# Adding the weights onto the low-rank part by accumulating transfers from GpSimd's queue instead of by a GpSimd sum

## Chip, core and metric

The kernel runs on one core of one Trainium2 chip. The metric is the device time of one launch in microseconds (us). Before the change it is 2744.04 us, the median of three runs (2742.25 to 2744.21).

The engines are named as in the profile: PE (TensorE, matrix products), DVE (VectorE), ACT (ScalarE), POOL (GpSimd) and SP (SyncE, which here only issues transfers). "SPq", "ACTq" and "POOLq" are the transfers that those engines issue.

## What is computed

The reference quantizes a weight matrix with a low-rank addition to the nearest of 32 codebook values, group by group, multiplies by it, and passes the result through a second linear layer with a small mixture of experts:

```
lora_delta = lora_B @ lora_A * (32.0 / 64.0)
scale      = exp(scale_log)                        # one per row and group of 128 columns
normalized = (weight + lora_delta).reshape(O, I // 128, 128) / scale
idx        = searchsorted(thresholds, normalized)  # 31 thresholds, 32 values
quantized  = cb[idx]
w          = (quantized - normalized) + normalized
w_eff      = (w * scale).reshape(O, I) + lora_delta
h          = x @ w_eff.T                           # x: 4096 x 2048, w_eff: 2048 x 2048
out        = x + ffn(h)                            # W_base, bias, router, experts
```

All of it is in float32. The change is in the sum `weight + lora_delta`.

## The kernel before

The kernel has two stages. Stage 1 (to about 1210 us of the span) builds the product of the two weight matrices, so that stage 2 has to multiply `x` only once; it does that with a two-level Strassen scheme and PE sets its pace. The change is in stage 1 alone.

**Strips.** Stage 1 goes over 16 strips of 128 columns. For strip `i` there is a tile `w_i` (128 partitions x 16 groups x 128, 1 MB), which becomes the normalized weight, and a tile `a_i` of the same size, which becomes the quantized weight and then PE's stationary operand. Each strip is handled in two halves `f` of 8 groups (128x1024 elements). There are two buffers for `w`, three for `a`, two for the mask `above`, and one in PSUM for the low-rank product `d`.

**One strip's quantization** is 28 steps (line 460; the lowest three thresholds are done elsewhere). In each step ACT writes a mask `above` = relu(w - threshold) (L462) and DVE copies the next codebook step into `a` where the mask is not zero (L463). With two masks, ACT can write the mask of step k+2 only when DVE has finished the copy of step k.

**Everything else is threaded between the steps.** The scheduler is off (`manual_schedule`), so the order of each engine's queue is the order of the program. `behind(k, ...)` puts work behind step k of the running strip i (k = 0 to 27): on ACT it then stands after the mask of step k, on DVE after its copy, on PE, POOL and SP just in that order. What is put there while strip i is quantized:

- PE: `delta(i+1, 0)` at the start and `delta(i+1, 1)` at step 7 (L408): the low-rank product of the next strip's halves, both into the one PSUM tile `d`, so that half 1 has to wait until half 0 has been read. Between them the products of strip i-1 with the second weight matrix (L526, `products`, at steps 2, 5, 8, 11, then 17, 20, 22), the first of which waits for POOL's line 479 of strip i-1. The tiles of `m` have three PSUM buffers, so a new one waits for ACT to copy an old one out (L545, `keep`, at steps 5, 6, 17 and 19).
- SP: `load_w(i+1)` (L343, 1 MB) at step 3, and the pieces of the second weight matrix (L395).
- ACT: `scaled(i+1, 0)` at step 7 and `scaled(i+1, 1)` at step 11 (L424), which copy 0.5 x `d` from PSUM into the halves of `a_{i+1}`.
- POOL: `normalize(i+1, 0)` at step 8 and `(i+1, 1)` at step 11: `w += a` (L431), then `w *= 1/scale` (L433).
- ACT: `level_0(i+1, f)`, three instructions for the lowest threshold (L441, L444, L446), at steps 10, 12, 14 for half 0 and 16, 18, 20 for half 1. L441 reads the normalized `w`, so it waits for L433. POOL then does the next two thresholds (`more_levels`, L453 and L454, at steps 14 and 20).
- After the strip, POOL's `straight_through(i)` (L477 to L479, three instructions for each half).
- While strips 5 to 14 run, POOL also makes a block of stage 2's operands: `outer_w` at step 4 (L280, four instructions), two `inner_pair` at step 9 (L289 to L292, eight instructions) and two more at step 15. SP stores them (L311 to L313). Strip 15 makes two such blocks, but has no next strip.

Strip 0 is started on its own: its low-rank part is added by DVE (L429), before the loop. `load_w(0)` and `load_w(1)` are issued at the start of the kernel (L360, L363).

Of the kernel before, what the change touches and what calls it, by code (L numbers as in the profile page):

```python
# [9 lines left out]
F32 = mybir.dt.float32  # L10
# [4 lines left out]
ALU = mybir.AluOpType  # L15
# [4 lines left out]
P = 128  # L20
BIG = 3.0e38
LORA_SCALE = 32.0 / 64.0
# [100 lines left out]
def exp_exact(nc, work, out, x):  # L123


    shape = list(x.shape)
    v = nc.vector
    v.tensor_scalar(x, x, -87.0, 88.0, ALU.max, ALU.min)
    k = work.tile(shape, F32, name="exp_k")
    half = 1.5 * 2.0**23  # L130
    v.tensor_scalar(k, x, 1.44269504088896341, half, ALU.mult, ALU.add)
    v.tensor_scalar(k, k, half, None, ALU.subtract)
    r = work.tile(shape, F32, name="exp_r")
    v.scalar_tensor_tensor(r, k, -0.693359375, x, ALU.mult, ALU.add)
    v.scalar_tensor_tensor(r, k, 2.12194440e-4, r, ALU.mult, ALU.add)
    y = work.tile(shape, F32, name="exp_y")
    v.tensor_scalar(y, r, 1.9875691500e-4, None, ALU.mult)
    for c in (1.3981999507e-3, 8.3334519073e-3, 4.1665795894e-2, 1.6666665459e-1, 5.0000001201e-1):
        v.scalar_tensor_tensor(y, y, c, r, ALU.add, ALU.mult)
    v.tensor_tensor(y, y, r, ALU.mult)  # L140
    v.tensor_tensor(y, y, r, ALU.add)

    bits = work.tile(shape, I32, name="exp_bits")
    v.tensor_scalar(bits, k, 127.0, float(1 << 23), ALU.add, ALU.mult)
    v.scalar_tensor_tensor(out, y, 1.0, bits.bitcast(F32), ALU.add, ALU.mult)
# [3 lines left out]
def adaln_ffn_kernel(  # L149
# [29 lines left out]
    nc = tc.nc  # L179
    D, N = xT.shape  # L180
    NS, _, NM, _ = weight.shape
# [34 lines left out]
    strip = [j * NK + k for k in range(NK) for j in range(4)]  # L216
# [44 lines left out]
    def columns(g, b, up, more):  # L261
        cols[g, b] = {
            "up": up.rearrange("p (j b a c) -> p j b a c", j=4, b=2, a=2),
            "more": more.rearrange("p (j b a c) -> p j b a c", j=3, b=2, a=2),
        }
# [50 lines left out]
    with ExitStack() as sa:  # L316
# [10 lines left out]
        wpool = sa.enter_context(tc.tile_pool(name="wpool", bufs=2))  # L327
# [11 lines left out]
        strips = {}  # L339

        def load_w(i):
            w = wpool.tile([P, NM, P], F32, tag="w", name=f"w_{i}")
            nc.sync.dma_start(w, weight[strip[i]])  # L343
            strips.setdefault(i, {})["w"] = w

        def load_la(i):
            la = lap.tile([2 * R, P], F32, tag="la", name=f"la_{i}")
            for h in range(2):
                nc.sync.dma_start(la[h * R : h * R + R], lora_A[:, ts(strip[i], P)])
            strips.setdefault(i, {})["la"] = la  # L350

        with tc.tile_pool(name="tables", bufs=1) as tables:
            log = tables.tile([P, NS * NM], F32, name="log")
            nc.scalar.dma_start(log, scale_log.rearrange("p s m -> p (s m)"))
            for h in range(2):
                nc.scalar.dma_start(
                    lora_BT_sb[h * R : h * R + R], lora_BT.rearrange("r (f h n p) -> r h f n p", h=2, n=4, p=P)[:, h]
                )
            nc.sync.dma_start(cb, codebook.partition_broadcast(P))
            load_w(0)  # L360
            for i in range(3):
                load_la(i)
            load_w(1)  # L363
            exp_exact(nc, tables, scale.rearrange("p s m -> p (s m)"), log)
            nc.vector.reciprocal(rscale, scale)
            neg_t, step, base = quantizer_tables(nc, tables, const, psum_t, cb)
# [47 lines left out]
        def half(i, f, t):  # L414
            return strips[i][t][:, ts(f, NM // 2), :]

        def new_a(i):
            strips[i]["a"] = apool.tile([P, NM, P], F32, tag="a", name=f"a_{i}")

        def scaled(i, f):  # L420

            if f == 0:
                new_a(i)
            nc.scalar.mul(half(i, f, "a"), strips[i]["d"], LORA_SCALE)  # L424

        def normalize(i, f):
            w = half(i, f, "w")
            if i == 0:
                nc.vector.scalar_tensor_tensor(w, strips[i]["d"], LORA_SCALE, w, ALU.mult, ALU.add)  # L429
            else:  # L430
                nc.gpsimd.tensor_tensor(w, w, half(i, f, "a"), ALU.add)  # L431
            r = rscale[:, strip[i], ts(f, NM // 2)]
            nc.gpsimd.tensor_tensor(w, w, r.unsqueeze(2).to_broadcast([P, NM // 2, P]), ALU.mult)  # L433

# [171 lines left out]
        def products(i, bs, c):  # L606

            for b in bs:
                multiply(i, b, c)
            if c == NC - 1:  # L610
                low_rank(i, bs)
# [9 lines left out]
        for i in range(NS):  # L621
            at = {}

            def behind(r, f, *args):
                at.setdefault(r, []).append(lambda: f(*args))

            if i > 1:

                products(i - 2, (3, 1), NC - 1)
                route(i - 2)  # L630
                behind(5, keep, i - 2, 3)
                behind(6, keep, i - 2, 1)
            if i + 1 < NS:
                delta(i + 1, 0)
                if i > 0:
                    behind(3, load_w, i + 1)
                behind(7, scaled, i + 1, 0)
                behind(8, normalize, i + 1, 0)
                for f, (a, b, c) in enumerate(((10, 12, 14), (16, 18, 20))):
                    behind(a, level_0, i + 1, f, 0)  # L640
                    behind(b, level_0, i + 1, f, 1)
                    behind(c, level_0, i + 1, f, 2)
                    behind(c, more_levels, i + 1, f)
                behind(11, scaled, i + 1, 1)
                behind(11, normalize, i + 1, 1)
            if i > 0:


                behind(9, load_route, i - 1)
                for c in range(2):  # L650
                    behind(2 + 3 * c, products, i - 1, (2, 0), c)
                if i + 1 < NS:
                    behind(7, delta, i + 1, 1)
                for c in range(2, NC):
                    behind(2 + 3 * c, products, i - 1, (2, 0), c)
                behind(13, multiply_router, i - 1)
                behind(17, keep, i - 1, 2)
                behind(19, keep, i - 1, 0)
                for c in range(NC - 1):
                    behind((17, 20, 22)[c], products, i - 1, (3, 1), c)  # L660
                behind(22, keep_router, i - 1)
                if i + 2 < NS:
                    behind(20, load_la, i + 2)
            else:
                behind(7, delta, i + 1, 1)
                behind(22, lora_columns, 0)
                behind(24, lora_columns, 1)
                behind(26, lora_router)
            for n, (g, b) in enumerate(made.get(i, [])):
                step_of = (4, 9, 11, 12, 15, 26, 27) if len(made[i]) == 1 else (  # L670
                    (4, 6, 8, 9, 10, 12, 13) if n == 0 else (17, 19, 21, 22, 23, 25, 26)
                )

                def begin(g, b):
                    columns(
                        g, b,
                        ypool.tile([P, 2048], F32, tag="up", name=f"up_{g}_{b}"),
                        ypool.tile([P, 1536], F32, tag="more", name=f"more_{g}_{b}"),
                    )
                    fetch(g, b)  # L680

                def inner_pair(g, b, ms):
                    z = zp.tile([P, 1024], F32, tag="z", name=f"z_{g}_{b}_{ms[0]}")
                    inner_some(nc.gpsimd, g, b, ms, z)

                behind((0, 14)[n], begin, g, b)
                r = step_of
                behind(r[0], outer_w, nc.gpsimd, g, b)
                behind(r[1], inner_pair, g, b, PAIRS[0])
                behind(r[1], inner_pair, g, b, PAIRS[1])  # L690
                behind(r[2], put, g, b, PAIRS[0])
                behind(r[3], put, g, b, PAIRS[1])
                behind(r[4], inner_pair, g, b, PAIRS[2])
                behind(r[4], inner_pair, g, b, PAIRS[3])
                behind(r[5], put, g, b, PAIRS[2])
                behind(r[6], put, g, b, PAIRS[3])
            quantize(i, at)
            straight_through(i)
# [448 lines left out]
```

## Time and profile before

One profiled execution took 2743.94 us, of which 2742.2 us are the span that the profile covers.

| | value |
|---|---|
| time, median of 3 runs | 2744.04 us |
| time of the profiled execution, its span | 2743.94 us, 2742.2 us |
| granted TensorE clock, mean | 0.967 |
| POOL busy over the span | 1244.1 us (45%) |
| DMA engines' mean share of queue 1 (SP) | 60.0% |
| POOL's sums L431 `w<-w,a`, 128x1024 | 30 of 2376 ns, 71.3 us |
| POOL's L433 `w<-w,rscale`, 128x1024 | 32 of 1896 ns, 60.7 us |
| ACT's L424 `a<-d`, 128x1024 | 30 of 1002 ns, 30.1 us |

The last three rows are groups of instructions by line, engine and tiles: how many there are, the mean duration of one, and the busy time together. How to read the views: a group's row ends with the idle time of its engine just before its instructions and with what ended that idle time. The list of waits says who waited for whom, with the total, the number of times and the longest. The timeline gives the instructions in order of time; an "x8" is eight merged ones, and brackets hold the idle time before. In the timeline an engine's next instruction often starts slightly before the last one's printed end.

### The profile page before, as it was taken

The numbers are of one execution on the slowest core, as the hardware profiler recorded it, in microseconds if no ns is written. First come the engines' busy times: TensorE is split into PE (matmuls) and PEld (weight loads), VectorE is DVE, ScalarE is ACT, GpSimd is POOL, SyncE is SP. The second block draws the span as 40 slices with busy tenths as digits, with TensorE's granted clock in tenths as the row PEclk, the third lists the DMA queues.
The fourth block names the chain that finished last, engine by engine and source line by source line (L and its number), as shares of the span: only waits on it lengthen the run. The fifth ranks groups of instructions, "written<-read, shape, count | busy, mean of one in ns | idle before, by whom it ended". The sixth has DMA issues, their size and how long they took to land.

```text
span 2742.2 us, 26226 instructions
## 1 busy us (share of the span) xinstructions
PE 2566.7 (94%) x10544; PEld 1766.2 (64%) x10544; DVE 1588.7 (58%) x993; ACT 1118.2 (41%) x741; POOL 1244.1 (45%) x699
## 2 busy tenths in 40 slices
PE   1599999999999999999599999999999999999999
PEld 0244444444444444445488888888888888888887
DVE  7999999999999999972433222332222422223321
ACT  3888989898888888840000000000000000000000
POOL 1666668888888888730203231032320323301314
PEclk9799999999999999999799999999999999999999
DMA  6345556767676666697954567545485455754564
GB/s 225 123 177 185 176 178 216 243 231 244 232 246 229 228 228 215 228 307 241 316 205 149 200 210 267 183 175 209 169 306 185 169 206 178 269 207 175 181 199 166
DMA packets 239913, 581.06 MB, mean 212 GB/s; under 512 B 18312, under 2 KB 140560, under 8 KB 194736
## 3 DMA queue, kind: packets, MB, share of 16 engines
q1 hardware_dynamic: 236848, 565.50, 60.0%
q10 hardware_dynamic: 2016, 11.14, 1.1%
q0 software_dynamic: 928, 2.75, 0.3%
q8 instruction: 83, 1.36, 0.2%
q14 instruction: 38, 0.31, 0.0%
HBM read 477.62 MB, written 101.71 MB: 211 GB/s over the span
## 4 chain that ended last, share of the span: by engine, by line
PE 56%; DVE 24%; ACT 10%; DMA 4%; issue 3%; SPq 3%; POOL 1%; DVEq 0%; POOLq 0%; ACTq 0%
PE z L805 48%; DVE a L463 22%; ACT above L462 7%; PE m L526 5%; PE z L835 1%; SPq L313 1%; ACT sg L441 1%; SPq L311 1%; SPq L312 1%; ACT sg L444 1%; ACT a L446 1%; ACT out L545 1%; DMA s_dram<-z 1%; DMA wbp<-in_wbT 0%; DMA first<-wc_dram 0%
## 5 line engine op out<-in xcount | busy, mean ns | idle before, releaser
L463 DVE COPY_PREDICATED a<-above,step 128x2048 f32<-128x2048 uint16 x449 | 1112.5, 2481 | 48.6 <-ACT above L462 5.7
L462 ACT ACTIVATE above<-w,neg_t 128x2048 bf16<-128x2048 f32 x449 | 895.2, 1999 | 127.9 <-DVE a L463 124.4
L805 PE MATMUL z<-t,s 128*128 128x256 f32 x3584 | 791.4, 380 | 0.4 <-DMA s<-s_dram 0.4
L805 PEld LDWEIGHTS z<-t,s 128*128 128x128 f32 x3584 | 678.3, 190 | 102.9 <-issue 12.5
L526 PE MATMUL m<-wbp,a 128*128 128x512 f32 x1024 | 505.2, 640 | 43.8 <-POOL a L479 35.2
L526 PE MATMUL m<-wb,a 128*128 128x512 f32 x1024 | 468.8, 601 | 26.9 <-ACT out L545 26.8
L526 PEld LDWEIGHTS m<-wbp,a 128*128 128x128 f32 x1024 | 205.7, 206 | 294.0 <-issue 242.8
L526 PEld LDWEIGHTS m<-wb,a 128*128 128x128 f32 x1024 | 195.5, 192 | 277.9 <-issue 239.2
L885 ACT COPY m<-z 128x1024 f32<-128x1024 f32 x28 | 28.4, 1013 | 769.8 <-PE z L805 769.8
L805 PE MATMUL z<-xA,s 128*128 128x256 f32 x1152 | 260.2, 385 | 33.5 <-DMA s<-s_dram 33.5
L805 PEld LDWEIGHTS z<-xA,s 128*128 128x128 f32 x1152 | 222.7, 194 | 66.0 <-issue 35.0
L896 POOL TENSOR_TENSOR c<-u,m 128x1024 f32<-128x1024 f32 x16 | 50.1, 3130 | 442.9 <-DVE u L893 400.4
L453 POOL TENSOR_SCALAR lv<-w,base 128x1024 f32<-128x1024 f32 x60 | 226.7, 3778 | 3.6
L896 POOL TENSOR_TENSOR M<-u,m 128x1024 f32<-128x1024 f32 x8 | 25.6, 3205 | 363.0 <-DVE u L893 358.3
L805 PE MATMUL z<-xC,s 128*128 128x256 f32 x768 | 169.7, 379 | 0.0
L805 PE MATMUL z<-xB,s 128*128 128x256 f32 x768 | 169.7, 379 | 0.0
L887 DVE TENSOR_TENSOR u<-z,m 128x1024 f32<-128x1024 f32 x28 | 34.2, 1223 | 218.6 <-issue 175.1
L805 PEld LDWEIGHTS z<-xB,s 128*128 128x128 f32 x768 | 146.1, 190 | 19.7
L805 PEld LDWEIGHTS z<-xC,s 128*128 128x128 f32 x768 | 146.0, 190 | 19.7
L891 ACT COPY m<-z 128x1024 f32<-128x1024 f32 x28 | 28.3, 1011 | 308.5 <-PE z L805 308.5
L454 POOL TENSOR_TENSOR a<-a,lv 128x1024 f32<-128x1024 f32 x60 | 142.5, 2375 | 18.5 <-ACT a L446 13.9
L477 POOL TENSOR_TENSOR a<-a,w 128x1024 f32<-128x1024 f32 x30 | 71.3, 2376 | 142.8 <-DVE a L463 142.8
(178 smaller groups left out, 1886.2 us busy)
## 6 DMA issues: line engine op xcount, KB each, us to landing
s<-s_dram SPq DMA_DIRECT2D x196, 1024.0 KB, 4.8
wbp<-in_wbT SPq DMA_DIRECT2D x131, 1024.0 KB, 5.2
xs<-in_xT SPq DMA_DIRECT2D x64, 512.0 KB, 7.1
xA<-in_xT SPq DMA_DIRECT2D x24, 1024.0 KB, 9.0
s_dram<-z SPq DMA_DIRECT2D x84, 256.0 KB, 5.6
w<-in_weight SPq DMA_DIRECT2D x16, 1024.0 KB, 7.4
xB<-in_xT SPq DMA_DIRECT2D x16, 1024.0 KB, 7.9
outT<-M SPq DMA_DIRECT2D x16, 1024.0 KB, 10.3
```

Of the source, the lines that this page charges most:

```text
L311: q.dma_start(to[:, n, 1:3, g, c], y[:, n, 1])
L453: v.tensor_scalar(lv, half(i, f, "w"), base[:, c + 1 : c + 2], base[:, c : c + 1], ALU.is_gt, ALU.mult)
L454: v.tensor_tensor(a, a, lv, ALU.add)
L462: nc.scalar.activation(above, q, AF.Relu, bias=neg_t[:, r : r + 1])
L463: nc.vector.copy_predicated(a, above.bitcast(U16), step[:, r : r + 1].to_broadcast([P, F]))
L477: v.tensor_tensor(a, a, w, ALU.subtract)
L526: nc.tensor.matmul(ps, strips[i]["a"][:, CM * c + m, :], t[:, m, :], start=c == 0 and m == 0, stop=False)
L805: nc.tensor.matmul(z[:, c, :], s[:, k, ts(c, P)], rhs[:, k, :], start=not more and k == 0 and c % PER == 0, stop=k == NK - 1 and c % PER = ...
L885: nc.scalar.copy(temp("m1", o), z["a"])
L887: nc.vector.tensor_tensor(temp("u2", o), z["b"], state["m1", o], ALU.add)
L891: nc.scalar.copy(temp("m5", o), z["c"])
L896: lambda d: nc.gpsimd.tensor_tensor(d, state["u3", o], state["m5", o], ALU.add),
```

## The change

`load_w` for strips 1 to 15 goes away, together with POOL's sum L431. ACT now writes the scaled low-rank part into `w` itself, and a transfer issued by POOL adds the 512 KB of the half's weights onto it. There are 30 such transfers, two for each of the strips 1 to 15. The buffer of `w_{i+1}` is taken when `scaled(i+1, 0)` runs. POOL's queue holds the issue where `scaled` stands; `normalize` keeps only the multiplication, which waits for the transfer.

Some of the steps change: `scaled(i+1, 1)` goes from step 11 to 9, `normalize(i+1, 0)` from 8 to 10, and `level_0(i+1, 0)` from steps 10, 12, 14 to 12, 14, 15 (with `more_levels(i+1, 0)` going from 14 to 15). Half 1's steps of `level_0` stay. Behind the diff, lines after 424 are two higher than before: the mask is L464, the copy L465, the multiplication by 1/scale L435, the scaled copy L425 and the transfer L426.

```
             load_w(0)
             for i in range(3):
                 load_la(i)
-            load_w(1)
...
             if f == 0:
                 new_a(i)
-            nc.scalar.mul(half(i, f, "a"), strips[i]["d"], LORA_SCALE)
+                strips[i]["w"] = wpool.tile([P, NM, P], F32, tag="w", name=f"w_{i}")
+            w = half(i, f, "w")
+            nc.scalar.mul(w, strips[i]["d"], LORA_SCALE)
+            nc.gpsimd.dma_start(w, weight[strip[i]][:, ts(f, NM // 2), :], accum_op=ALU.add)
...
             if i == 0:
                 nc.vector.scalar_tensor_tensor(w, strips[i]["d"], LORA_SCALE, w, ALU.mult, ALU.add)
             else:
-                nc.gpsimd.tensor_tensor(w, w, half(i, f, "a"), ALU.add)
+                pass
...
                 delta(i + 1, 0)
-                if i > 0:
-                    behind(3, load_w, i + 1)
                 behind(7, scaled, i + 1, 0)
-                behind(8, normalize, i + 1, 0)
-                for f, (a, b, c) in enumerate(((10, 12, 14), (16, 18, 20))):
+                behind(10, normalize, i + 1, 0)
+                for f, (a, b, c) in enumerate(((12, 14, 15), (16, 18, 20))):
...
-                behind(11, scaled, i + 1, 1)
+                behind(9, scaled, i + 1, 1)
                 behind(11, normalize, i + 1, 1)
```

## The prediction

> **What bounds the kernel now.** I read the groups of the page first, then the waits of stage 1 (0 to 1200 us), then one strip in the timeline, then the transfers. The two costliest groups:
>
> ```profile
> L463 DVE COPY_PREDICATED a<-above,step 128x2048 f32<-128x2048 uint16 x449 | 1112.5, 2481 | 48.6 <-ACT above L462 5.7
> L462 ACT ACTIVATE above<-w,neg_t 128x2048 bf16<-128x2048 f32 x449 | 895.2, 1999 | 127.9 <-DVE a L463 124.4
> ```
>
> DVE's copies take 1112.5 us. The 48.6 us of idle time before them are 0.1 us for each of 449 and 5.7 us of waiting for a mask. So stage 1 is DVE copying without a gap, and everything else fits in beside it. The waits say the same from the other side:
>
> ```profile
> POOL a L477 <- DVE a L463: 142.8, 15, 11.1
> ACT above L462 <- DVE a L463: 123.3, 235, 0.7
> PE m L526 <- ACT out L545: 31.1, 21, 2.1
> DVE a L463 <- ACT above L462: 5.7, 19, 0.7
> ```
>
> POOL is idle for 8 to 11 us at the end of every strip until DVE is done. ACT waits for DVE 0.5 us at a time: a copy comes every 2.58 us, a mask takes 2.00. ACT therefore can do about 1.1 us of other work between two masks before a copy is late, and gains back about 0.6 us in each step. Now the strip that starts at 486.1 us (rows out of the timeline of all engines):
>
> ```profile
> 486.12 2.38 POOL L477 TENSOR_TENSOR a<-a,w 128x1024 f32<-128x1024 f32 x1 [8.78 <-DVE a L463]
> ...
> 497.81 1.90 POOL L479 TENSOR_TENSOR a<-a,scale 128x1024 f32<-128x1024 f32 x1
> 498.17 0.57 ACT L545 COPY out<-m 128x512 f32<-128x512 f32 x1
> ...
> 498.78 3.70 PE L526 MATMUL m<-wb,a 128*128 128x512 f32 x8 [2.08 <-ACT out L545]
> ...
> 503.32 1.01 ACT L424 ACTIVATE a<-d 128x1024 f32<-128x1024 f32 x1
> 503.49 1.30 POOL L280 TENSOR_TENSOR more<-up,more 128x512 f32<-128x512 f32 x1
> ...
> 506.60 2.00 ACT L462 ACTIVATE above<-w,neg_t 128x2048 bf16<-128x2048 f32 x1 [0.39 <-DVE a L463]
> ...
> 509.28 1.16 PE L408 MATMUL d<-la,lora_BT_sb 64*128 64x128 f32 x16
> ...
> 511.10 1.13 ACT L441 ACTIVATE sg<-w,neg_t 128x1024 bf16<-128x1024 f32 x1
> ...
> 514.03 1.00 ACT L424 ACTIVATE a<-d 128x1024 f32<-128x1024 f32 x1
> ```
>
> I count from the strip's start: 486.1 is 0. POOL's straight-through ends at 13.6 and `outer_w` at 18.7. ACT scales half 0 at 17.2 (step 7) and half 1 at 27.9 (step 11). PE makes the second `d` from 23.2 to 24.3, far ahead of step 11. It can't be earlier: PE's queue holds before it two rounds of products, and the second product waits until ACT has copied an old tile out at step 5 (12.0 to 12.6), then needs 3.5 + 7.0 us of PE.
>
> **The change part by part.**
>
> *Removed: POOL's 30 sums, 30 x 2.376 = 71.3 us.* Worth 0: POOL waits for DVE at the end of every strip in any case, and DVE's waits for the whole chain over ACT are 5.7 us, which bounds the gain. *Removed: SP's load at step 3 and the one at the start.* Worth 0: SP issues in 0.35 us; at the start DVE's tables, not a transfer, decide until 32.7 us.
>
> *Moved: `scaled(.,1)` from step 11 to step 9.* ACT's mask of step 9 ends at 508.5, that is 22.4, and the next instruction is now the scaled copy, which needs the `d` that PE finishes at 24.3. Step 7's copy released that PSUM tile long before; it is PE's products that are late. So ACT waits 1.9 us, copies until 25.4, and only then writes the mask of step 10, ready at 27.3. DVE wants it at ten copies after the start, 10 x 2.577 = 25.8. The copy is 1.55 us late. PE starts this `d` 23.0 to 23.4 after the start of the strip in ten of the strips 1 to 14, at 23.9 in strip 1, and at about 25 in strips 4, 9 and 14, where a product runs slowly (5.40 us for 3.70). Sum: 14 x 1.55 = 21.7, and 0.8 + 0.5 + 2.0 + 1.7 + 1.7 = 6.7 for the late ones: **28.4 us**. Strip 0 has no products before its `d`: 0.
>
> *Added: issues on POOL.* The trace has 16 transfers issued by POOL, of 0.55 to 0.95 us each on its queue; I take 0.75. The first issue has room (17.2 + 1.0, or 18.7 behind `outer_w`). The second waits for ACT until 25.4, and in strips 5 to 14 two `inner_pair` (eight instructions from 510.15 to 515.90: 5.75 us) stand behind it, and behind them the multiplication of half 0. So: 25.4 + 0.75 + 5.75 + 1.90 = 33.8 for a normalized half 0. ACT reaches `level_0` at step 12, some 31.7 after the start with the delay above counted in. It waits 2.1 us; that the copy of step 13 is late by 1.85 follows as before. 10 x 1.85 = **18.5 us**. In strips 1 to 4 there is no `inner_pair`, and half 0 is ready when its transfer has landed.
>
> *Moved: `level_0`.* Steps 15 and 16 now hold 1.13 and 1.03 us of ACT back to back instead of with a step between. By the rule above (1.1 us to spare, 0.6 back in each step) the copies of steps 16, 17, 19 and 21 are late by about 0.75 together; the same count over the old order gives 0.4, and the page has 5.7 / 15 = 0.38. 15 x 0.37 = **5.5 us**.
>
> *Added: the landing time L of an accumulating transfer of 512 KB.* No row has one. The nearest, from the list of transfers (KB each, median us from issue to landing):
>
> ```profile
> xs<-in_xT SPq DMA_DIRECT2D x64, 512.0 KB, 7.1
> s_dram<-z SPq DMA_DIRECT2D x84, 256.0 KB, 5.6
> w<-in_weight SPq DMA_DIRECT2D x16, 1024.0 KB, 7.4
> ...
> s_dram<-lz SPq DMA_DIRECT2D x12, 256.0 KB, 2.5
> ...
> s_dram<-lz POOLq DMA_DIRECT2D x6, 256.0 KB, 6.8
> ```
>
> Below, L is not under 5.7, the shortest of POOL's. Above, 6.8 us doubled for the bytes and doubled again because the target has to be read too: 27. Size alone costs little here (5.6, 7.1 and 7.4 us for 256, 512 and 1024 KB), so I take 6.8 + 1.5, and 0.3 to 1.8 for the second read: L = 9. In strips 1 to 4 half 0 is in time up to L = 31.7 - 1.9 - 18.3 = 11.5, in strips 5 to 14 up to 33.8 - 1.9 - 18.7 = 13.2. At 9 the transfer costs nothing. Beyond 13 every us costs 15 us; at 27 it would be some 200.
>
> POOL's sums L431 take 2364 to 2391 ns each in stage 1, beside copies that fill 96% of DVE's time (69.0 us of each 72), while the same form takes 3130 ns in stage 2 (L896): these copies do not seem to hold POOL up. A rule speaks against this all the same: the Trainium skill (SBUF — State Buffer, "Who interferes with whom") says that GpSimd's descriptor generation is starved while DVE runs in a mode that takes the port pair both share, and advises the hardware queues. By it, with each issue blocked for one copy, L would be 2.5 us longer, and 11.5 would still cost nothing; by the row it stays 9.
>
> **Sum:** 28.4 + 18.5 + 5.5 = 52.4 us. On the profiled execution's own 2743.94 us (span 2742.2 and 1.7 around it, 0.1 under the median of the runs): **2796 us**. PE's stage 2 only starts later.
>
> **The rivals.**
>
> *Slow transfers (slower still).* L is above 13 us, and then ACT's wait at step 12 is set by landing, not by POOL's queue. For it: POOL's 256 KB land in 6.8 us where SP's take 2.5 for the same tile, and the DMA engines are about 70% busy in strips 5 to 15. Against: size costs little. At L = 16: 15 x 2.8 = 42 more, 2838 us.
>
> *The waits are hidden (no change).* ACT's masks would have to be two steps ahead, or PE's `d` 2 us earlier. For it: the longest wait of DVE for a mask is only 0.7 us, so ACT's detours are swallowed now. Against: PE's order and the copy at step 5 don't change. 2744 us.
>
> *Faster.* One mechanism: DVE's copies come closer together when POOL reads less beside them. In strip 0, with POOL idle, masks follow each other in 2.54 us (51.78, 54.32, 56.86), later in 2.58. If that is POOL's doing and its sums decide it, 420 copies x 0.04 = 17 us, and the 5.7 of waits: 2721 us. It decides only if step 9 waits for less than the 1.1 us that ACT has to spare. Against: with POOL idle at 478 to 486 us the distance is still 2.57.
>
> **How the numbers follow.** Forecast 0.65, slow transfers 0.22, hidden 0.06, faster 0.07. The forecast's own range is 2775 (only the first wait, without the three slow strips and half the second: 21.7 + 9.2 = 31) to 2812 (L up to 14). The range reaches to L = 16 above: 2772 to 2838. It leaves out the last two cases and the end of the second, about 2 in 10. A change under 0.2%, or 5.5 us, cannot be told from none here. Slower 0.87, same 0.06, faster 0.07.
>
> **What would show it.** The waits of after: ACT's scaled copy on PE's `d`, 14 times about 2 us; ACT's L443 on POOL's L435 in strips 5 to 14, about 2 us each; DVE's waits for masks near 58 us instead of 5.7; strips of about 74.5 us (1 to 4) and 76.5 us (5 to 14) instead of 72.4. POOL's transfers land in about 9 us; a multiplication that waits for its transfer with POOL idle in strips 5 to 14 would mean the first rival. If the copies stay at 72.4 us a strip, I am wrong about what ACT has to spare.

## The result, and the profile after

The changed kernel takes **2806.63 us** (median of 4 runs, 2804.11 to 2807.28) against 2743.14 us before (4 runs in the same session): a ratio of 1.0231, 95% interval 1.0213 to 1.0248, some 63 us slower. The profiled execution's span is 2805.5 us at a granted clock of 0.957. The same two groups of instructions as before, from the page of the changed kernel (L465 is the copy, L464 the mask):

```profile
L465 DVE COPY_PREDICATED a<-above,step 128x2048 f32<-128x2048 uint16 x449 | 1109.5, 2475 | 114.7 <-ACT above L464 77.0
L464 ACT ACTIVATE above<-w,neg_t 128x2048 bf16<-128x2048 f32 x449 | 893.1, 1998 | 127.0 <-DVE a L465 123.7
```

The copies take 3 us less than before, but the idle time before them has grown from 48.6 to 114.7 us, and 77.0 of it is now waiting for a mask (5.7 before). All of the loss is there: DVE starts on its own straight-through of the last strip at 1272.6 us instead of 1209.8, 62.8 us later, and the span is 63.3 us longer. The two rows, before and after:

```profile
1209.76 1.20 DVE L477 TENSOR_TENSOR a<-a,w 128x512 f32<-128x512 f32 x1
1272.58 1.13 DVE L479 TENSOR_TENSOR a<-a,w 128x512 f32<-128x512 f32 x1
```

Who makes ACT late is in the waits of stage 1. Before (0 to 1210 us), one row had ACT waiting for PE or POOL:

```profile
ACT sg L441 <- POOL w L433: 23.2, 3, 18.3
```

After (0 to 1260 us):

```profile
POOL w L426 <- ACT w L425: 147.9, 20, 24.3
...
DVE a L465 <- ACT above L464: 77.0, 72, 3.8
ACT sg L443 <- POOL w L435: 47.2, 12, 18.5
...
ACT w L425 <- PE d L407: 39.6, 14, 3.9
...
POOL w L435 <- DMA w<-in_weight: 16.2, 6, 4.1
```

Of ACT's rows one is new and one has grown. It waits 14 times for PE's low-rank product `d`, 39.6 us (1.9 to 3.9 us each), and 12 times instead of 3 for POOL's multiplication. Of the 47.2 us there, 23 belong to strip 0's start, as before; the other ten are of 2.4 us each. POOL itself waits for a transfer only 6 times. In one strip, the one whose straight-through starts at 500.5 us, that looks like this. First POOL's timeline:

```profile
519.11 0.90 POOL L426 DMA_DIRECT2D w<-in_weight  x1
527.92 0.86 POOL L426 DMA_DIRECT2D w<-in_weight  x1 [7.91 <-ACT w L425]
528.49 1.05 POOL L289 TENSOR_TENSOR z<-up 128x256 f32<-128x256 f32 x1
...
533.89 0.72 POOL L292 TENSOR_TENSOR z<-up,z 128x256 f32<-128x256 f32 x1
534.58 3.75 POOL L435 TENSOR_TENSOR w<-w,rscale 128x1024 f32<-128x1024 f32 x2
```

Half 0's transfer is issued at 519.1 and lands 5.4 us later, but its multiplication starts at 534.6: POOL stands 7.91 us at the second issue, waiting for ACT, and then makes eight `inner_pair` instructions. Then ACT and DVE in their timelines (an "x3" is three copies, and the brackets stand before the first):

```profile
526.60 1.02 ACT L425 ACTIVATE w<-d 128x1024 f32<-128x1024 f32 x1 [3.61 <-PE d L407]
...
536.50 1.15 ACT L443 ACTIVATE sg<-w,neg_t 128x1024 bf16<-128x1024 f32 x1 [2.44 <-POOL w L435]
```

```profile
529.55 7.63 DVE L465 COPY_PREDICATED a<-above,step 128x2048 f32<-128x2048 uint16 x3 [3.47 <-ACT above L464]
539.58 10.21 DVE L465 COPY_PREDICATED a<-above,step 128x2048 f32<-128x2048 uint16 x4 [2.40 <-ACT above L464]
550.27 5.05 DVE L465 COPY_PREDICATED a<-above,step 128x2048 f32<-128x2048 uint16 x2 [0.48 <-ACT above L464]
```

Each of ACT's waits comes out at DVE about one copy later: 3.47 us for the one at step 9, 2.40 for the one at step 12. The transfers themselves are in the list of issues of the changed kernel:

```profile
xs<-in_xT SPq DMA_DIRECT2D x64, 512.0 KB, 9.0
...
w<-in_weight POOLq DMA_DIRECT2D x30, 512.0 KB, 5.8
```

They land in 5.8 us, quicker than transfers of the same size on SP's queue in the same execution.

### The profile page after: what moved, and what is told of

It is laid out like the page before. It is cut to its first block, busy times and chain, and to the rows that moved or that the text cites. A ratio compares the mean times of both kernels' runs of the same rounds, so it can differ in the third digit from the quotient of the medians.

```text
span 2805.5 us, 26173 instructions
## 1 busy us (share of the span) xinstructions
PE 2567.7 (92%) x10544; PEld 1766.1 (63%) x10544; DVE 1585.7 (57%) x993; ACT 1118.8 (40%) x741; POOL 1200.0 (43%) x699
## 3 DMA queue, kind: packets, MB, share of 16 engines
q0 software_dynamic: 5248, 18.48, 3.9%
## 4 chain that ended last, share of the span: by engine, by line
PE 58%; DVE 18%; ACT 11%; POOL 4%; issue 4%; DMA 3%; SPq 2%; DVEq 0%; POOLq 0%; ACTq 0%
PE z L805 47%; DVE a L465 16%; PE m L528 8%; ACT above L464 7%; PE z L835 1%; ACT a L448 1%; POOL w L435 1%; ACT out L547 1%; DMA xs<-in_xT 1%; POOL z L290 1%; SPq L312 1%; POOL z L289 1%; PE d L407 1%; POOL z L291 1%; POOL z L292 1%
## 5 line engine op out<-in xcount | busy, mean ns | idle before, releaser
L465 DVE COPY_PREDICATED a<-above,step 128x2048 f32<-128x2048 uint16 x449 | 1109.5, 2475 | 114.7 <-ACT above L464 77.0
L464 ACT ACTIVATE above<-w,neg_t 128x2048 bf16<-128x2048 f32 x449 | 893.1, 1998 | 127.0 <-DVE a L465 123.7
L528 PE MATMUL m<-wb,a 128*128 128x512 f32 x1024 | 475.7, 609 | 28.2 <-ACT out L547 28.2
L885 ACT COPY m<-z 128x1024 f32<-128x1024 f32 x28 | 28.4, 1013 | 769.1 <-PE z L805 769.1
## 6 DMA issues: line engine op xcount, KB each, us to landing
xB<-in_xT SPq DMA_DIRECT2D x16, 1024.0 KB, 10.1
```

Source lines behind the costliest of these rows:

```text
L464: nc.scalar.activation(above, q, AF.Relu, bias=neg_t[:, r : r + 1])
L465: nc.vector.copy_predicated(a, above.bitcast(U16), step[:, r : r + 1].to_broadcast([P, F]))
L528: nc.tensor.matmul(ps, strips[i]["a"][:, CM * c + m, :], t[:, m, :], start=c == 0 and m == 0, stop=False)
L885: nc.scalar.copy(temp("m1", o), z["a"])
```

## The experiments

The theory is that two waits in queue order cost the time: ACT at step 9 for a product that PE makes too late, and ACT at step 12 for a multiplication that POOL's queue holds up; a small rest is crowding of ACT's steps. The rival is that the accumulating transfers, or their descriptors on POOL, cost it. In the edits "+" and "-" stand against the changed kernel unless the text says otherwise.

**Only the steps moved, with the sum kept (e6_order).** Against the kernel before:

```
-                behind(8, normalize, i + 1, 0)
-                for f, (a, b, c) in enumerate(((10, 12, 14), (16, 18, 20))):
+                behind(10, normalize, i + 1, 0)
+                for f, (a, b, c) in enumerate(((12, 14, 15), (16, 18, 20))):
...
-                behind(11, scaled, i + 1, 1)
+                behind(9, scaled, i + 1, 1)
```

> The kernel before with GpSimd's sum and SP's loads kept, and only the steps moved as the change moves them (scaled half 1 to step 9, normalize half 0 to step 10, level_0 of half 0 to steps 12, 14, 15). My theory (ACT waits at step 9 for PE's second low-rank product): ACT's waits for it are there 14 times, about 2 to 4 us each, and the time is 2743 + 36 + 6 = 2785 us (2776 to 2795). Rival (the accumulating transfers and GpSimd's descriptor work cost the time): 2743 to 2749 us.

Measured: 2780.55 us, ratio 1.0134 (1.0119 to 1.0149) to before. Its waits:

```profile
DVE a L463 <- ACT above L462: 46.7, 61, 3.4
...
ACT a L424 <- PE d L408: 33.5, 14, 3.6
...
ACT sg L441 <- POOL w L433: 22.5, 2, 18.1
```

Without a single accumulating transfer 37 of the 63 us are there, with the same 14 waits for PE. The wait for POOL's multiplication is absent (the 22.5 us are strip 0's): no issue that waits for ACT stands ahead of it here. So the step that was moved, not the transfer, makes the larger part.

**PE's product earlier (e1_split), inner_pair later (e2_pool), and both (e3_both).** One edit for each of the two waits. PE makes `d` between the two products of round 1, and POOL's `inner_pair` goes behind the multiplication of half 0:

```
-                for c in range(2):
-                    behind(2 + 3 * c, products, i - 1, (2, 0), c)
+                behind(2, products, i - 1, (2, 0), 0)
+                behind(5, products, i - 1, (2,), 1)
                 if i + 1 < NS:
                     behind(7, delta, i + 1, 1)
+                behind(7, products, i - 1, (0,), 1)
                 for c in range(2, NC):
```

```
-                step_of = (4, 9, 11, 12, 15, 26, 27) if len(made[i]) == 1 else (
+                step_of = (4, 10, 11, 12, 15, 26, 27) if len(made[i]) == 1 else (
```

> The changed kernel, with PE making the second low-rank product between the two products of round 1 instead of behind both, so 3.5 us earlier. My theory: ACT's wait at step 9 goes, its 36 us with it, the wait at step 12 stays: 2771 us (2764 to 2778). Rival (the transfers set the pace): no change, 2800 to 2810 us.

> The changed kernel, with the two inner_pair of strips 5 to 14 put behind the multiplication of half 0 instead of ahead of it. My theory: ACT's wait at step 12 goes, 10 x 2.3 us, the wait at step 9 stays: 2784 us (2779 to 2789). Rival (transfers are late, not GpSimd's queue): the wait at step 12 stays, 2800 to 2808 us.

> Both moves together (PE's product earlier and inner_pair later). My theory: 2806 - 36 - 23 = 2747 us (2743 to 2756), DVE's waits for masks down to about 10 us. Rival (a third cost lies in the transfers): 2765 us or more.

| kernel | median, us | ratio to before (95%) | DVE waits for masks, us | ACT waits for PE's `d`, us | ACT's L443 waits for POOL's L435, us |
|---|---|---|---|---|---|
| changed | 2806.63 | 1.0231 (1.0213 to 1.0248) | 77.0 | 39.6 | 47.2, 12 times |
| PE earlier | 2769.21 | 1.0094 (1.0079 to 1.0109) | 35.5 | 1.3 | 44.4, 12 times |
| inner_pair later | 2780.07 | 1.0132 (1.0115 to 1.0148) | 48.0 | 34.0 | 22.3, 2 times |
| both | 2750.07 | 1.0022 (1.0013 to 1.0031) | 16.5 | 0.8 | 22.9, 2 times |

Each edit removes its own wait and leaves the other, and all three times lie where the theory put them. In the row "both" DVE's waits for masks came down to 16.5 us, not to the 10 expected. The transfers are all still there in it, in the same number and with nearly the same landing time (6.0 us for 5.8), and 57 of the 63 us are gone.

**The move undone (e4_back).** Half 1's scaled copy stands at step 11 again; its multiplication goes to step 14:

```
-                behind(9, scaled, i + 1, 1)
-                behind(11, normalize, i + 1, 1)
+                behind(11, scaled, i + 1, 1)
+                behind(14, normalize, i + 1, 1)
```

> The changed kernel with one move undone: scaled half 1 back at step 11 (so inner_pair is ahead of the second issue in GpSimd's queue, and so is the multiplication of half 0), and the multiplication of half 1 at step 14, as its transfer is issued later. My theory: both waits go, without any change to PE's order, and only the crowding of level_0 is left: 2750 us (2745 to 2757). Rival (the transfers or their issue cost by themselves): 2760 us or more.

Measured: 2750.95 us, ratio 1.0027 (1.0016 to 1.0037). Here POOL does wait for transfers, and it costs nothing:

```profile
POOL w L435 <- DMA w<-in_weight: 142.8, 20, 10.6
...
DVE a L465 <- ACT above L464: 18.8, 58, 1.5
```

POOL stands 142.8 us waiting for transfers to land, up to 10.6 us at a time, and DVE's waits are still at 18.8 us. POOL has that time to spare, and ACT doesn't ask for the result before step 12 or 16. The transfers land later here than in the changed kernel, up to 11.4 us after their issue (7.5 there): in the strip where one took 10.1 us (from 590.5 us) the DMA engines were busy all the time, with SP's loads beside it (share 1.00), in one where it took 7.1 (from 663.3 us) the share was 0.77. So up to these lengths the landing time is not on the path; what is, is the place of an instruction behind another engine's late work.

**Transfers that copy (e5_plain).** `accum_op` is taken out, so the low-rank part is missing from what is quantized:

```
-            nc.gpsimd.dma_start(w, weight[strip[i]][:, ts(f, NM // 2), :], accum_op=ALU.add)
+            nc.gpsimd.dma_start(w, weight[strip[i]][:, ts(f, NM // 2), :])
```

> The changed kernel with transfers that copy instead of adding, so that the low-rank part is left out of the weights that are quantized. My theory (queue order costs, not the adding): 2806 us (2803 to 2810), waits of ACT at steps 9 and 12 as in the changed kernel, landing no more than 1 us shorter than the 5.8 us of the adding ones. Rival (adding makes the transfers late): under 2795 us.

Measured: 2801.22 us, ratio 1.0206 (1.0192 to 1.022), 2 us under the expected band, and the transfers land 1.7 us sooner (4.1 us for 5.8), not at most 1. The expectation was wrong in both, but the rival would need under 2795. The two profiled executions differ by 9.6 us (2797.66 and 2807.28), and their timelines show most of it. The issue takes 0.53 us on POOL's queue instead of 0.86 for the second half's, ahead of `inner_pair`, and ACT's wait at step 12 goes from 2.43 to 2.11 us: about 10 x 0.33 = 3.3 us. And PE has a slow product in 4 of the strips 1 to 14 here and in 7 in the changed kernel's profile (more on this below), 1.7 us each: 5.1 us. The medians differ by 5.4 us; how many slow products the executions without a profile had is not known.

**What is left, and the best order (e7_spread, e8_sum).** In the run of both, 6.6 us were left. With `level_0` spread to where ACT has a step between (e7_spread, on top of both edits), and the same order of steps with the sum and SP's loads of before (e8_sum):

```
-                for f, (a, b, c) in enumerate(((12, 14, 15), (16, 18, 20))):
+                for f, (a, b, c) in enumerate(((11, 13, 15), (18, 20, 22))):
```

> Both moves of the previous run of both (PE's product between the two of round 1, inner_pair behind the multiplication of half 0) and level_0 spread to steps 11, 13, 15 and 18, 20, 22. My theory (what is left of the 6.6 us is crowding of ACT's steps 15 to 20): DVE's waits for masks fall from 16.5 to under 5 us and the time to 2740 us (2736 to 2745), level with the kernel before or a little under it. Rival (the transfers cost the rest): it stays at 2750 us.

> The same order of steps as in the run with level_0 spread, but with GpSimd's sum and SP's loads of the kernel before. My theory (neither sum nor transfer is on the path once the queues are in order): the same time as that run within 4 us, 2740 us (2736 to 2745). Rival (the transfers free GpSimd for something that counts): at least 6 us slower than the run with transfers.

Measured: **2740.71 us** with the transfers, ratio 0.9987 (0.9978 to 0.9995) to before, and 2741.13 us with the sum, ratio 0.999 (0.9981 to 0.9999). DVE's waits for masks are at 1.1 us in the one, and 1.6 in the other. Both are a little faster than the kernel before, by 3.8 and 3.4 us, where DVE's waits for masks are down by 4.6 and 4.1 us from 5.7. They don't differ from each other: in a good order GpSimd's 30 sums and the 30 transfers cost the same, nothing that shows. The page of the kernel with transfers (e7_spread), for the copy:

```profile
L465 DVE COPY_PREDICATED a<-above,step 128x2048 f32<-128x2048 uint16 x449 | 1110.8, 2477 | 45.6 <-ACT above L464 1.1
```

What remains before the copies is 0.1 us each. From its first copy (at about 49 us) on, stage 1 has little left to gain without fewer or faster copies.

## Why the prediction was right

The forecast, 2796 us, is 10.6 us under the measured time, and its direction and both places hold. DVE's timeline over stage 1 gives the first two terms: the brackets before a copy, less the 0.1 us that stand before every copy. The third is what is left of the added idle time (114.7 - 48.6 = 66.1 us).

| term | predicted, us | measured, us |
|---|---|---|
| step 9: scaled copy waits for PE's `d`, strips 1 to 14 | 28.4 | 36.3 (14 waits of 1.6 to 3.7) |
| step 12: `level_0` waits for POOL's queue, strips 5 to 14 | 18.5 | 22.9 (10 waits of 2.3) |
| crowding of `level_0` | 5.5 | about 7 |
| copies themselves | 0 | -3 (1109.5 for 1112.5) |
| sum | 52.4 | 63 |

**Step 9** was mis-sized in one assumption: that the late products would stay in the strips 4, 9 and 14. Each such strip costs 1.7 us more, as predicted, but in the changed kernel there are seven of them (4, 6 to 9, 13 and 14), and 4 x 1.7 = 6.8 of the 7.9 us are that. PE's timeline shows the slow product, behind the same wait for ACT's copy at step 5 as in a fast strip (the changed kernel, strip at 500.5 us):

```profile
513.20 5.40 PE L528 MATMUL m<-wb,a 128*128 128x512 f32 x8 [2.08 <-ACT out L547]
518.43 3.60 PE L528 MATMUL m<-wbp,a 128*128 128x512 f32 x8
...
525.39 1.16 PE L407 MATMUL d<-la,lora_BT_sb 64*128 64x128 f32 x16
```

A wait of 1.8 to 2.1 us stands there in every one of the strips 2 to 14. What differs is where it falls. In stage 1 of all ten profiles PE's granted clock is either 1 or 0.5, and it changes only at times that lie a whole number of 3.41 us apart; these stretches begin at another point in every profile. Here are three of them around the wait in this strip, and three around the wait of 2.10 us in the strip at 423.9 us, where the product took 3.70 us (after the times: length, PE's busy time, granted clock, share of the DMA engines, GB/s):

```profile
510.70:514.10 3.40, 1.32 (x3) 1.00 0.59 171
514.10:517.50 3.40, 3.40 (x5) 0.50 0.57 217
517.50:520.90 3.40, 3.40 (x9) 1.00 0.15 11
432.10:435.50 3.40, 2.38 (x6) 1.00 0.04 5
435.50:438.90 3.40, 2.32 (x6) 1.00 0.92 330
438.90:442.30 3.40, 3.40 (x10) 1.00 0.13 51
```

In the first the wait lies whole in one stretch, and PE gets half the clock in the next one; in the second a border cuts the wait in two, and nothing is lost. In the changed kernel each of the seven slow strips has 1.89 us or more of the wait in one stretch, and the six others have at most 1.85; over the ten profiles it is 1.86 or more in the 44 slow ones and at most 1.98 in the 86 others (between these two figures both occur). A strip of 72.4 us is 21.2 stretches long, so the wait moves on by a fifth of a stretch each time: before the change every fifth strip was slow. A slow strip of the changed kernel is 78.3 us, or 22.95 stretches, so that the wait hardly moves, and 6 to 9 are slow in a row. The number of slow strips is in part chance, 3 to 7 in these profiles.

**Step 12** was mis-sized in what lies between ACT's copy and the normalized half 0: 0.75 + 5.75 + 1.90 = 8.40 us in the sum, 8.87 measured in each of the ten strips. 0.30 us of that is the time from the end of ACT's copy to the start of the issue, which the sum left out (527.62 to 527.92 above). Another 0.15 is the issue with the eight `inner_pair` instructions, 6.65 us instead of 6.50: the issue is printed with 0.86 us and the first instruction behind it with 1.05 instead of 0.73, but that one starts 0.30 us before the issue's end. With them each wait is 0.4 us longer.

**The removed work** was worth what was said, nothing: with the order mended, the kernel with GpSimd's sum and the one without it take the same time. **The landing time** was taken as 9 us and measured 5.8 (5.3 to 7.5), at the lower bound and in part under it; up to 11.5 it made no difference to the sum, so the error cost nothing, and the rival of slow transfers had no ground. The rule on descriptor generation that was set against the rows gives no visible cost here: 30 issues took 0.86 to 1.06 us each, beside copies that leave DVE idle for about 0.1 us between two, and the longest landed after 7.5 us. Whether DVE's copies run in the mode that the rule speaks of, no run here shows.

**The rival "hidden"** failed where its own text put the doubt: ACT waits 1.9 to 3.9 us for `d`, more than the 1.1 us that it has to spare. **The rival "faster"** has its answer in the last two runs, which differ in the sums, loads and transfers alone: a copy takes 2477 ns with the transfers and 2479 with GpSimd's sums, 0.7 us over all 449, where that rival had 17.

The signs that the prediction named came out: strips of 74.5 to 74.7 us (1 to 3) and of 76.6 to 76.7 (5 and 10 to 12), where no product was slow, and 14 and 10 new waits of ACT. DVE's waits for masks are 77.0 us, not 58. What was not tried: an edit that moves PE's wait against the stretches of the clock, so that part is read from the ten profiles alone.

## What to carry to other kernels

Where one engine sets the pace and the others are threaded between its steps by hand, the cost of an edit can lie not in the work that it removes or adds but in which instruction now stands behind which: an instruction that is moved two steps earlier can be waiting for an engine that has not got there yet, and all that follows it in its queue waits too. Putting a transfer's issue on a compute engine's queue puts a wait there as well; look at what stands behind it. Before moving a consumer earlier, find when its producer ends in the timeline, not only when its input could be ready.

## What the runs showed of the hardware

- A transfer of 512 KB that adds, issued by GpSimd, landed in 5.8 us, and the same transfer as a copy in 4.1 us (medians; up to 11.4 us where the DMA engines were fully busy). The software queue's share of the DMA engines was 3.9% and 2.2% for the same 5248 packets and 18.48 MB, or 1.9 times when the 0.3% of the other GpSimd transfers is taken off both; in the other runs with adding transfers the share was 3.5% to 3.8%, which makes it 1.7 to 1.8 times. The Trainium skill (Collectives: The Full Stack, "The bandwidth ceiling: the fold count and why AG ≠ RS ≠ AR") says of ReduceScatter that it is slower than a copying AllGather because the add needs two source reads, with a measured ratio of 1.93. The ratio here is of that size; that a second read is its reason no run here shows.
- An accumulating issue occupies GpSimd's queue for 0.86 to 1.06 us, a copying one for 0.53 to 0.77. Behind an accumulating one the next GpSimd instruction starts 0.3 us before the issue's printed end and is printed 0.3 us longer; with `inner_pair` behind it, the copying issue saves 0.33 us.
- PE's eight matmuls took 5.40 us instead of 3.70 right behind an idle time of 2 us in 7 of the strips 2 to 14 (3 before). In the changed kernel these are the strips where 1.89 us or more of the idle time lay in one stretch of 3.41 us of the granted clock; the next stretch was then granted 0.5.
